# Cross-attention with image prompts: where the context is transposed, and how the last heads' prompts reach the output

## The chip, the core and the metric

The kernel runs on one core of a Trainium2 chip. The metric is device time of one execution, in microseconds (us); lower is better. The engines are named as the profile names them: PE is TensorE (PEld its weight loads), DVE is VectorE, ACT is ScalarE, POOL is GpSimd, and SP is SyncE, which here only issues DMAs.

## The reference

Everything is fp32. There are B = 8 batches, S = 112 queries of C = 320 channels, H = 20 heads of 16 channels, and a context of 375 tokens of E = 512 features. The first 371 tokens are text, the last 4 are image prompts.

```
text_ehs, ip_ehs = ehs[:, :-4], ehs[:, -4:]
q = heads(x @ W_q); k_t = heads(text_ehs @ W_k); v_t = heads(text_ehs @ W_v)
probs_t  = softmax(q @ k_t^T * 16**-0.5)
text_out = probs_t @ v_t
k_ip = heads(ip_ehs @ W_k_ip); v_ip = heads(ip_ehs @ W_v_ip)
qsem = l2norm(probs_t @ text_ehs)              # one 512-vector per query and head
sem  = qsem @ l2norm(ip_ehs)^T
probs_ip = softmax(q @ k_ip^T * 16**-0.5 + 0.5 * sem) * spatial_mask
out = (text_out + probs_ip @ v_ip) @ W_out + b_out + x
```

The context holds one batch in (8, 375, 512); the mask has one number per query.

## The kernel before

**What is computed per step.** A step is one pair (batch b, group g); a batch has five groups of four heads. The kernel never forms qsem. It keeps, per batch, the matrix of inner products of all context tokens with each other (the gram matrix G, text and normalised prompts) in a buffer `u`, with a column of ones and the values v of each head beside it. For each head, `multiplied` (L641) computes p^T times [G | prompts | 1 | v] on PE, where p are the unnormalised probabilities: 12 blocks of 32 tokens for four heads, so 48 matmuls a step, in four PSUM banks `ps_qd`. `reduced` (L687, DVE) multiplies the first 371 columns with p and sums them, which is the squared length of qsem; `value_sums` (L654, ACT) copies the last 21 columns (four prompt products, the sum of p, 16 channels of p times v).

**What makes p.** `scores` (L592, PE) computes one head's scores two steps ahead (LEAD = 2): heads 2 and 3 behind product block 0 of a step, heads 0 and 1 behind block 6. `probabilities` takes the maximum on DVE (nmx, L605), the exponential on ACT (p, L609), and sends p by a DMA on SP's queue into `xg`, with 28-row pieces; `transposed` (L622) then turns `xg` into `xgT` by one DVE transpose of 128x1536, which works in squares of 32x32, and PE loads `xgT` as weights in the next step's products. The order of DVE in a step is: nmx of heads 2 and 3, xgT, nmx of heads 0 and 1, four reductions.

**What stands between two steps.** Behind each step's products, `between(b, g)` issues PE work for the next batch nb = b + 1 and closes batch b - 1. Generators are advanced by pieces with `run`. Before the change the PE order behind the products of batch b is:

| g | PE work behind the products |
|---|---|
| 0 | three gram blocks of nb (L415) |
| 1 | values of nb, token blocks 0 and 1 (L486) |
| 2 | values of nb, token block 2; key block 0 (L453) |
| 3 | key block 1; in odd b transposes of x for a pair of batches; key block 2 (three PE transposes of `k3`, L444); transposes of attn (`ps_a`, L845); in even b queries (L305) |
| 4 | context transposes of nb + 1, first token block (`ps_c`, L357); output projection of b - 1 (`ps_o`, L858); context transposes, blocks 1 and 2; queries |

**The context.** `load_ctx(b)` reads a batch's 375x512 floats into `ct` with token rows on partitions, in four DMAs of up to 128 rows. It is called by `load_next(b + 2)` behind the step (b, 0). `transposed_context` turns `ct` into `ctxT` (features on partitions) by four PE transposes per token block through a PSUM bank, copied out by ACT. The gram, the keys and the values all read `ctxT`. `load_embed` loads the weights W_k, W_v and the prompt weights so that feature e * 128 + p lies in row p of block e. POOL fills the last columns of `ctxT` (memset in `begin`) and copies the normalised prompts into its columns 371 to 374 (in `gram`).

**Closing a batch.** `finish(b)` runs in ten pieces while the next batch is computed: the root of the squared lengths (ACT), the fused prompt scores and their softmax (DVE and ACT), w (L771, DVE), then on POOL the product of w with the prompt values `vip` (wv, L827), two sums (L838, L839) and the last sum into `attn` (L840). Then come PE transposes of attn (`ps_a`), an ACT copy (aT), the output projection (`ps_o`), DVE's sum with x and bias (`ob`), and the store.

**What sets the order.** PE, SP, DVE and, behind the prologue, ACT run in the order in which the program issues the work. POOL's order is made by a scheduler up to the last batch, and by hand in it. PSUM has eight banks: four `ps_qd`, two `ps_sc` (the scores; `bank(..., spare=True)` borrows from them), two `ps_mm` (the rest). A tile of a ring must wait until the tile that held the place before has been read.

**The last batch and the end.** The last batch, b = 7, has no next batch, so its work is shared between ACT, POOL and DVE (`shared`), and its heads close in two parts: `finish(b, (0, 16), bd=...)` for the first 16 heads, and `finish(b, (16, 20), nc.vector, late=True)` for the last group. The first part does not multiply w with prompt values. It transposes w (`ps_wT`) and multiplies it on PE with `bd`, a matrix with the prompt values of each head in that head's channels, into the same bank as the transposes of attn. The second part multiplies w with `vip` on DVE, adds the sum to attn and then transposes. `awake(3, end=True)` issues three idle matmuls before the last reductions.

Of the kernel before, what the change touches and what calls it, by code (L numbers as in the profile page):

```python
# [14 lines left out]
NIP = 4  # L15
# [5 lines left out]
def kernel(  # L21
# [36 lines left out]

    GROUP = 4
# [54 lines left out]
    def load_embed(eng, t, w):  # L114
        eng.dma_start(t[:, :, :C], w.rearrange("(e p) f -> p e f", p=P))
# [7 lines left out]

    def load_ctx(b):
        ct = io.tile([P, NT, E], F32, tag="ct", name=f"ct_{b}")
        for c in range(NT):
            rows = min(P, T - c * P)
            some = rows - rows % 16
            nc.sync.dma_start(ct[:some, c, :], ehs[b, c * P : c * P + some, :])
            if some < rows:  # L130
                nc.sync.dma_start(ct[some:rows, c, :], ehs[b, c * P + some : c * P + rows, :])
        return ct
# [82 lines left out]
    def normalised_prompts():  # L215
# [16 lines left out]
        for src, dst, n in ((ipn, ipnT, "n"), (ip_sb, ipT, "r")):  # L232
            ps = bank(f"ps_ipT{n}")
            for e in range(NE):
                nc.tensor.transpose(
                    ps[:, e * N : (e + 1) * N], src[:, e * P : (e + 1) * P], ident[:N, :N]
                )
            nc.vector.tensor_copy(
                dst, ps[:, : NE * N].rearrange("p (e n) -> p e n", n=N)
            )  # L240
# [87 lines left out]
    def begin(b):  # L328
        s = st[b] = dict(ct=loaded.pop(b))
        s["ctxT"] = work.tile([P, NE, TP], F32, tag="ctxT", name=f"ctxT_{b}")  # L330
        nc.gpsimd.memset(s["ctxT"][:, :, T:], 0.0)

        s["kT"] = work.tile([P, NC, T], F32, tag="kT", name=f"kT_{b}")
        s["vext"] = work.tile([P, NT, C + REST], F32, tag="vext", name=f"vext_{b}", bufs=1)
# [14 lines left out]
    def transposed_context(b):  # L349
        begin(b)  # L350
        s = st[b]
        ct, ctxT = s["ct"], s["ctxT"]
        for c in range(NT):
            rows = min(P, TT - c * P)
            ps = bank(f"ps_c_{b}_{c}", spare=b > 1 and c > 0)
            for e in range(NE):
                nc.tensor.transpose(  # L357
                    ps[:, e * P : e * P + rows],
                    ct[:rows, c, e * P : (e + 1) * P],
                    ident[:rows, :rows],  # L360
                )
# [72 lines left out]
    def keys(b):  # L434
# [3 lines left out]
        for i in range(NC):  # L438
            ps = bank(f"ps_k_{b}_{i}")
# [39 lines left out]
    def values(b):  # L479
        s = st[b]  # L480
        ctxT, vext = s["ctxT"], s["vext"]
# [201 lines left out]
    def reduced(b, g, a0=0):  # L683
        s = st[b]
        for a, (h, ps) in list(enumerate(zip(groups[g], s["qd", g])))[a0:]:
# [11 lines left out]
        del s["p", g]  # L697
# [5 lines left out]
    def finish(b, heads=(0, H), eng=None, late=False, bd=None):  # L703


        s = st[b]
        eng = eng or nc.gpsimd
# [14 lines left out]
        if not late:  # L722
            if "xb" not in s:
                s["xb"] = work.tile([S, C], F32, tag="xb", name=f"xb_{b}", bufs=1)
                with_bias(b)
# [86 lines left out]
        else:  # L812
            yield from prompt_sums_and_projection(
                b, s, eng, part, n, h0, h1, i0, i1, w, attn, ah, late
            )
# [9 lines left out]
    def prompt_sums_and_projection(b, s, eng, part, n, h0, h1, i0, i1, w, attn, ah, late):  # L825
# [7 lines left out]
        if late:  # L833
            ips = small.tile([S, GROUP, D], F32, tag="ips", name=f"ips_{b}", bufs=1)
            nc.vector.tensor_reduce(ips, wv.rearrange("p n h d -> p h d n"), AX.X, ALU.add)
            nc.vector.tensor_tensor(ah, ah, ips, ALU.add)
        else:
            eng.tensor_tensor(wv[:, :2], wv[:, :2], wv[:, 2:], ALU.add)  # L838
            eng.tensor_tensor(ah, ah, wv[:, 0], ALU.add)  # L839
            eng.tensor_tensor(ah, ah, wv[:, 1], ALU.add)  # L840
        yield

        ps = bank(f"ps_a_{b}_{h0}", spare=not late)
# [10 lines left out]
        if not late:  # L854
            s["o"] = bank(f"ps_o_{b}")
        ps = s["o"]
        for i in range(i0, i1):
            nc.tensor.matmul(  # L858
                ps[:S, :C], aT[:, i, :], wo_sb[:, i, :], start=(i == 0), stop=(i == NC - 1)
            )  # L860
        yield
# [7 lines left out]
    LEAD = 2  # L869
# [11 lines left out]
    def between(b, g):  # L881
# [26 lines left out]
        if g == 3:  # L908
            if new:
                run(("k", nb), None, 1)  # L910
            for bs in first if b > 0 else ():
                run(("q", bs[0]), lambda: project_queries(bs), 3)
            if b == 0:
                run(("t", b), lambda: prompt_logits(b))
            if nb < B - 1:
                run(("k", nb), None, 1)
            if b > 0 and new:
                run(("f", b - 1), None)
            for bs in rest:
                run(("q", bs[0]), None)  # L920
        if g == 4:
            if nb + 1 < B:
                run(("c", nb + 1), lambda: transposed_context(nb + 1))
            if b > 0 and new:
                run(("f", b - 1), None, 2)
            if nb + 1 < B:
                run(("c", nb + 1), None, 2)
# [51 lines left out]
    for n, (b, g) in enumerate(steps[:-NG]):  # L979
# [27 lines left out]
        if g == 0:  # L1007
            load_next(b + 2)
        elif g == 1:
# [39 lines left out]
    for g in range(NG):  # L1049
# [34 lines left out]
        if g == 1:  # L1084
            prompt_values(b)
# [4 lines left out]
        if g == 3:  # L1090
# [5 lines left out]
            for _ in range(3):  # L1096
                next(first)
    next(first)
    run(before, None)
    nc.scalar.preload_act_table(AF.Sqrt)  # L1100
    run(before, None)
    awake(3, end=True)
    run(before, None)
    reduced(b, g)
    value_sums(b, g)
    last = finish(b, (FULL * HC, H), nc.vector, late=True)
# [3 lines left out]
    next(first)  # L1110
    for _ in range(2):
        next(last)
    for _ in range(2):
        next(first)
    for _ in range(4):
        next(last)
    drain(gens[before])
    drain(first)
# [44 lines left out]
```

## Time and profile before

| what | value |
|---|---|
| median of 3 runs | 448.66 us (448.07 to 451.15) |
| the profiled execution | 449.23 us |
| its span from the first to the last record | 447.5 us |
| group products, PE L641 | 3840 matmuls, 217.9 us busy |
| all matmuls of PE | 5095 |
| nmx, DVE L605 | 160 of 529 ns |
| reductions, DVE L687 | 148 of 542 ns |
| exponentials, ACT L609 | 160 of 582 ns |
| wv, POOL L827 | 6 of 2461 ns |

The steps of a middle batch take PE 10.64, 10.72, 10.64, about 9.8 and 9.55 us for g = 0 to 4, some 51.3 us a batch. Of each step the 48 products with the four scores inside them take 5.37 us. The end, behind the last product at 432.9 us, runs through DVE's last reductions (to 435.97), the root on ACT with a table load (to 438.12), two rounds of transposes and projection on PE (to 444.13), the sum (444.65) and the store (447.5).

In the page, part 1 gives each engine's busy time, part 4 the shares of the chain that ended last, and part 5 the costliest groups: line, engine, operation, output<-input, count, then busy time and mean of one, then the idle time before them and what ended it. In the chain in order of time, a line gives the start, the length, the engine, the work and its line; in an engine's timeline, a line gives start, length, the instruction, and in brackets the idle time before it with what ended it.

### The profile page before, as it was taken

What the parts mean: (1) busy time and instruction counts of PE and PEld (TensorE: products, weight loads), DVE (VectorE), ACT (ScalarE), POOL (GpSimd) and SP (SyncE); (2) the same over time, 40 slices, a digit from 0 to 9 for tenths busy, and PEclk for the clock granted to TensorE, in tenths of its full rate; (3) what the DMA queues carried; (4) which work ended last, traced back from release to release, by engine and by line L of the source; (5) the groups of instructions that cost most, each with busy time, mean ns of one, the idle gap of its engine ahead of it and who ended that gap; (6) DMA issues with size and microseconds to landing.
All of it is one profiled execution on the core that took longest, in us unless ns stands there. A gap on an engine that the chain in (4) does not pass through costs nothing.

```text
span 447.5 us, 13078 instructions
## 1 busy us (share of the span) xinstructions
PE 435.1 (97%) x5095; PEld 336.3 (75%) x5095; DVE 308.9 (69%) x649; ACT 196.5 (44%) x664; POOL 111.1 (25%) x270
## 2 busy tenths in 40 slices
PE   8998999999999999999999999999999999999885
PEld 8756767888778876788777777778777887787782
DVE  4047356787687767786687866776677867878784
ACT  2254232435345353343535463333534454446782
POOL 4302201011150111511142121511133120527420
PEclk9999999999999999999999999999999999999998
DMA  7669955544645566544646466464556437454400
GB/s 237 174 170 259 212 138 141 141 136 139 171 123 135 145 171 167 128 130 142 167 123 158 117 174 163 129 158 149 141 159 147 137 87 196 123 134 112 136 2 26
DMA packets 52159, 64.84 MB, mean 145 GB/s; under 512 B 18370, under 2 KB 44146, under 8 KB 52098
## 3 DMA queue, kind: packets, MB, share of 16 engines
q1 hardware_dynamic: 51658, 63.45, 53.1%
q8 instruction: 40, 0.66, 0.7%
q10 hardware_dynamic: 440, 0.56, 0.4%
q14 instruction: 21, 0.17, 0.1%
HBM read 19.30 MB, written 5.32 MB: 55 GB/s over the span
## 4 chain that ended last, share of the span: by engine, by line
PE 86%; DVE 4%; ACT 4%; DMA 3%; issue 1%; POOL 1%; SPq 1%; DVEq 0%; POOLq 0%; ACTq 0%
PE ps_qd L641 39%; PE ps_v L486 13%; PE ps_g L415 8%; PE ps_k L453 8%; PE ps_s L592 4%; PE ps_q L305 3%; PE ps_o L858 3%; DMA xg<-p 3%; PE ps_c L357 2%; DVE xgT L622 2%; ACT p L609 2%; PE ps_g L387 1%; DVE junk L687 1%; PE ps_w L374 1%; PE ps_k L469 1%
## 5 line engine op out<-in xcount | busy, mean ns | idle before, releaser
L641 PE MATMUL ps_qd<-u,xgT 32*112 32x104 f32 (+11 forms) x3840 | 217.9, 352 | 3.4 <-DVE xgT L622 1.2
L641 PEld LDWEIGHTS ps_qd<-u,xgT 32*112 32x112 f32 x3840 | 185.8, 172 | 36.7 <-issue 10.3
L605 DVE TENSOR_REDUCE nmx<-ps_s 112x1 f32<-112x371 f32 x160 | 77.6, 529 | 72.4 <-PE ps_s L592 72.3
L622 DVE STREAM_TRANSPOSE xgT<-xg 128x1536 f32<-128x1536 f32 x40 | 119.0, 2976 | 8.0 <-DMA xg<-p 7.4
L609 ACT ACTIVATE p<-ps_s,nmx 112x371 f32<-112x371 f32 x160 | 86.9, 582 | 80.7 <-DVE nmx L605 58.0
L687 DVE CUSTOM_DVE_ANT_0 junk<-ps_qd,p 112x371 f32<-112x371 f32 x148 | 80.2, 542 | 15.8
L559 POOL COPY u<-vr 128x64 f32<-128x64 f32 x120 | 25.8, 236 | 163.9 <-PE ps_qd L641 106.5
L592 PE MATMUL ps_s<-kT,qm 32*112 32x375 f32 (+1 forms) x320 | 64.8, 481 | 0.4 <-ACT p L609 0.4
L486 PE MATMUL ps_v<-wv_sb,ctxT 128*128 128x384 f32 (+1 forms) x192 | 63.5, 480 | 0.0
L486 PEld LDWEIGHTS ps_v<-wv_sb,ctxT 128*128 128x128 f32 x192 | 35.2, 190 | 19.7
L453 PE MATMUL ps_k<-ctxT,wk_sb 128*128 128x371 f32 x136 | 45.9, 482 | 0.0
L654 ACT COPY pvs<-ps_qd 112x21 f32<-112x21 f32 x150 | 16.0, 188 | 64.3 <-PE ps_qd L641 63.4
L415 PE MATMUL ps_g<-ctxT 128*128 128x375 f32 (+2 forms) x168 | 37.4, 379 | 0.0
L453 PEld LDWEIGHTS ps_k<-ctxT,wk_sb 128*128 128x128 f32 x136 | 25.1, 190 | 15.3 <-issue 0.5
L415 PEld LDWEIGHTS ps_g<-ctxT 128*128 128x128 f32 x168 | 28.1, 190 | 8.4
L592 PEld LDWEIGHTS ps_s<-kT,qm 32*112 32x112 f32 x320 | 25.9, 170 | 5.7 <-ACT kT L460 2.1
L314 DVE TENSOR_SCALAR qm<-ps_q,emask 128x224 f32<-128x224 f32 (+1 forms) x25 | 9.2, 400 | 23.6 <-PE ps_q L305 23.6
L611 ACT COPY ipl<-ps_s 112x4 f32<-112x4 f32 x140 | 23.5, 168 | 0.0
L493 ACT COPY vext<-ps_v 128x384 f32<-128x384 f32 (+1 forms) x24 | 11.2, 466 | 25.4 <-PE ps_v L486 25.4
L460 ACT COPY kT<-ps_k 128x371 f32<-128x371 f32 x17 | 8.0, 470 | 25.3 <-PE ps_k L453 25.3
L403 ACT ACTIVATE ug<-ps_g 128x375 f32<-128x375 f32 (+2 forms) x24 | 9.0, 376 | 22.4 <-PE ps_g L415 17.9
L827 POOL TENSOR_TENSOR wv<-vip,w 112x1280 f32<-112x1280 f32 x6 | 14.8, 2461 | 14.6 <-DVE w L771 14.6
(131 smaller groups left out, 336.4 us busy)
## 6 DMA issues: line engine op xcount, KB each, us to landing
xg<-p SPq DMA_DIRECT2D x160, 162.3 KB
u<-ug SPq DMA_DIRECT2D x128, 99.0 KB
ct<-in_ctx_dram SPq DMA_DIRECT2D x16, 256.0 KB
vip<-vipd SPq DMA_DIRECT2D x7, 560.0 KB
vr<-vd SPq DMA_DIRECT2D x32, 120.0 KB
vd<-vext SPq DMA_DIRECT2D x7, 320.0 KB
ct<-in_ctx_dram SPq DMA_DIRECT2D x8, 224.0 KB
vd<-vext SPq DMA_DIRECT2D x7, 160.0 KB
```

The lines of the kernel that those rows point to most:

```text
L415: nc.tensor.matmul(ps[:, : T - t0], ctxT[:, e, t0 : t0 + P], ctxT[:, e, t0:T], start=(e == 0), stop=(e == NE - 1),)
L453: nc.tensor.matmul(ps[:, :TT], wk_sb[:, e, i * P : (i + 1) * P], s["ctxT"][:, e, :TT], start=(e == 0), stop=(e == NE - 1),)
L486: nc.tensor.matmul(ps[:, :w], ctxT[:, e, c * P : (c + 1) * P], wv_sb[:, e, :w], start=(e == 0), stop=(e == NE - 1),)
L559: nc.gpsimd.tensor_copy(region(b, c)[:, :, UV - c * P :], s["vr"][:, c * QN : (c + 1) * QN, g, :])
L592: nc.tensor.matmul(ps[:S, :w], qm[a * RG : (a + 1) * RG, i, r, j * S : (j + 1) * S], s["kT"][a * RG : (a + 1) * RG, i, :w], start=True, st ...
L605: nc.vector.tensor_reduce(nmx, ps[:S, :TT], AX.X, ALU.max, negate=True)
L609: nc.scalar.activation(p, ps[:S, :TT], AF.Exp, bias=nmx)
L611: nc.scalar.copy(s["ipl"][:, groups[g][a], :], ps[:S, TT:T])
L622: nc.vector.transpose(xT.rearrange("p j (k q) -> p q j k", q=QN), xg.rearrange("p q (j k) -> p q j k", k=RG),)
L641: nc.tensor.matmul(banks[a][:S, j * RG : UW], xT[a * RG : (a + 1) * RG, j, :S], region(b, c)[a * RG : (a + 1) * RG, q, q * RG :], start=(j ...
L654: nc.scalar.copy(s["pvs"][:, h, :], ps[:S, TT:UW])
L687: nc.vector.tensor_tensor_reduce(out=junk, in0=ps[:S, :TT], in1=s["p", g][:, a, :], scale=1.0, scalar=0.0, op0=ALU.mult, op1=ALU.add, accu ...
```

## The change

**The context of batches 2 to 7 is turned by DVE.** `load_ctx(b)` for b >= 2 lays the context out in squares: row i of a quarter a holds, for each of 12 blocks j of 32 tokens, token 32 j + i's features 128 a to 128 a + 127. That takes four DMAs of 32 x 11 x 128 floats and four of 19 x 128 for the last tokens, in pieces of 512 bytes, and a POOL memset of the last block. `transposed_context` for b >= 2 then issues three DVE transposes of 128x512, one per 128 tokens, that read every fourth element of a row; no PE transposes and no ACT copies are left there. Feature e + 4 p now lies in row p of block e, so `load_embed` loads the weights in that order, and the PE transposes that remain (contexts 0 and 1, and the prompts) read their input with a step of four elements (`chunk`).

**The places in `between` move.** The DVE transposes stand behind g = 0, 1 and 2 (g = 1, 2 and 3 in b = 0) instead of PE's in g = 4. In g = 3 the piece of `finish(b - 1)` that issues `ps_a` goes ahead of key block 1. Key block 2 moves from g = 3 to g = 4, behind `ps_o`, and takes a spare bank. The load of a context is issued behind (b, 4) for batch b + 3, with one first call behind (0, 0) for batch 2, instead of behind (b, 0) for batch b + 2. The memset of the padding in `ctxT` is left out for b >= 2, since the transposes write those columns.

**The last heads' prompts go through the projection on their own.** `projected_prompts` multiplies the last four heads' block of `bd` with W_out's last rows ahead of time (`bw`, 16 x 320). `last_heads` then adds to the output bank two matmuls: attn of the last heads (without prompts) times W_out, and w transposed times `bw`. The three idle matmuls at the end, the load of `vip` for the last batch and the `late` branch of `finish` go. The last reductions are issued in two parts, one before and three behind other work, and the ACT copies of the last products stand ahead of them.

```diff
 def load_embed(eng, t, w):
-    eng.dma_start(t[:, :, :C], w.rearrange("(e p) f -> p e f", p=P))
+    eng.dma_start(t[:, :, :C], w.rearrange("(p e) f -> p e f", e=NE))
...
+def chunk(t, e):
+    return t.rearrange("t (p e) -> t e p", e=NE)[:, e, :]
 def load_ctx(b):
     ct = io.tile([P, NT, E], F32, tag="ct", name=f"ct_{b}")
+    if b >= LEAD:
+        v = ct.rearrange("p c e -> p (c e)").rearrange("p (j f) -> p j f", f=P)
+        full = TT // RG
+        nc.gpsimd.memset(v[:, full, :], 0.0)
+        for a in range(QN):
+            nc.sync.dma_start(
+                v[a * RG : (a + 1) * RG, :full, :],
+                ehs[b, : full * RG, a * P : (a + 1) * P].rearrange("(j i) f -> i j f", i=RG),
+            )
+        for a in range(QN):
+            nc.sync.dma_start(
+                v[a * RG : a * RG + TT - full * RG, full, :],
+                ehs[b, full * RG : TT, a * P : (a + 1) * P],
+            )
+        return v
...
 def begin(b):
-    nc.gpsimd.memset(s["ctxT"][:, :, T:], 0.0)
+    if b < LEAD:
+        nc.gpsimd.memset(s["ctxT"][:, :, T:], 0.0)
...
 def transposed_context(b):
+    if b >= LEAD:
+        for c in range(NT):
+            some = slice(c * QN, (c + 1) * QN)
+            nc.vector.transpose(
+                ctxT[:, :, c * P : (c + 1) * P].rearrange("p e (j i) -> p j e i", i=RG),
+                ct[:, some, :].rearrange("p j (k e) -> p j e k", e=NE),
+            )
+            yield
+        return
     for c in range(NT):
-        ps = bank(f"ps_c_{b}_{c}", spare=b > 1 and c > 0)
+        ps = bank(f"ps_c_{b}_{c}")
...
 def keys(b):
-        ps = bank(f"ps_k_{b}_{i}")
+        ps = bank(f"ps_k_{b}_{i}", spare=0 < b < B - 1 and i == FULL)
...
+def projected_prompts(bd):
+    k0 = FULL * HC * NIP
+    k = HN - k0
+    ps = bank("ps_bT", spare=True)
+    nc.tensor.matmul(ps[:REST, :k], bd[k0:HN, FULL * P : C], ident[k0:HN, k0:HN], start=True, stop=True)
+    bT = work.tile([P, NC, S], F32, tag="aT", name="bT")
+    nc.scalar.copy(bT[:REST, 0, :k], ps[:REST, :k])
+    yield
+    ps = bank("ps_bw", spare=True)
+    nc.tensor.matmul(ps[:k, :C], bT[:REST, 0, :k], wo_sb[:REST, FULL, :], start=True, stop=True)
...
+    nc.scalar.copy(bw, ps[:k, :C])
+    yield
+def last_heads(b):
...
+    nc.scalar.activation(rn, rn, AF.Sqrt)
+    nc.scalar.preload_act_table(AF.Exp)
+    yield
...
+    nc.vector.scalar_tensor_tensor(w, ex, sm_sb, over_ip(rx), ALU.mult, ALU.mult)
+    yield
+    ps = bank(f"ps_a_{b}_{h0}")
+    nc.tensor.transpose(ps[:, :S], attn[:, FULL * P :], ident[:S, :S])
+    aT = work.tile([P, NC, S], F32, tag="aT", name=f"aT_{b}_{h0}")
+    nc.scalar.copy(aT[:, FULL, :], ps[:, :S])
+    nc.tensor.matmul(s["o"][:S, :C], aT[:, FULL, :], wo_sb[:, FULL, :], start=False, stop=False)
+    yield
+    k = n * NIP
+    ps = bank(f"ps_wT_{b}_{h0}")
+    nc.tensor.transpose(ps[:k, :S], w.rearrange("s h n -> s (h n)"), ident[:S, :S])
+    wT = small.tile([S, S], F32, tag="wTl", name="wT_last", bufs=1)
+    nc.scalar.copy(wT[:k], ps[:k, :S])
+    nc.tensor.matmul(s["o"][:S, :C], wT[:k], s["bw"], start=False, stop=True)
...
 def between(b, g):
     if g == 3:
+        if b > 0 and new:
+            run(("f", b - 1), None)
         if new:
             run(("k", nb), None, 1)
         for bs in first if b > 0 else ():
             run(("q", bs[0]), lambda: project_queries(bs), 3)
         if b == 0:
             run(("t", b), lambda: prompt_logits(b))
-        if nb < B - 1:
-            run(("k", nb), None, 1)
-        if b > 0 and new:
-            run(("f", b - 1), None)
         for bs in rest:
             run(("q", bs[0]), None)
+    if 0 <= g - (b == 0) < NT and nb + 1 < B:
+        run(("c", nb + 1), lambda: transposed_context(nb + 1))
     if g == 4:
-        if nb + 1 < B:
-            run(("c", nb + 1), lambda: transposed_context(nb + 1))
         if b > 0 and new:
             run(("f", b - 1), None, 2)
-        if nb + 1 < B:
-            run(("c", nb + 1), None, 2)
+        if nb < B - 1:
+            run(("k", nb), None, 1)
...
-    if g == 0:
+    if n == 0:
         load_next(b + 2)
-    elif g == 1:
+    if g == NG - 1:
+        load_next(b + 3)
+    if g == 1:
         gram_to_groups(b + 1, (1,))
...
+value_sums(b, g)
 next(first)
+late = projected_prompts(bd[:, 1])
 run(before, None)
+next(late)
+run(before, None)
+next(late)
+reduced(b, g, 0, 1)
+next(first)
+next(first)
 nc.scalar.preload_act_table(AF.Sqrt)
 run(before, None)
-awake(3, end=True)
-run(before, None)
-reduced(b, g)
-value_sums(b, g)
-last = finish(b, (FULL * HC, H), nc.vector, late=True)
+reduced(b, g, 1)
+next(first)
+last = last_heads(b)
```

## The prediction

> **What bounds the kernel now.** I read the page's busy times first, then the chain that ended last in order of time, then the timelines of POOL and DVE around one batch's end. One step is one pair (batch b, group g); steps of a batch differ only in what PE does behind its 48 group products.
>
> ```profile
> PE 435.1 (97%) x5095; PEld 336.3 (75%) x5095; DVE 308.9 (69%) x649; ACT 196.5 (44%) x664; POOL 111.1 (25%) x270
> ...
> PE 86%; DVE 4%; ACT 4%; DMA 3%; issue 1%; POOL 1%; SPq 1%; DVEq 0%; POOLq 0%; ACTq 0%
> ```
>
> PE is never idle for long between 37 and 405 us, so PE time removed there is worth its full length, unless a wait takes its place. The chain through g = 3 and g = 4 of batch 4:
>
> ```profile
> 286.55 2.69 PE ps_k L453 x8
> 289.24 0.32 PE ps_k L444 x3
> 289.56 0.29 PE ps_a L845 x3
> 289.85 1.35 PE ps_q L305 x6
> ...
> 296.56 0.59 PE ps_c L357 x4
> 297.15 1.61 PE ps_o L858 x6
> 298.77 0.83 PE ps_c L357 x8
> 299.60 1.15 PE ps_q L305 x6
> ```
>
> Columns are start, length, work. The reader is to see the order: in g = 3 (PE from 281.18; products end at 286.55) the second key block comes first and the transposes of attn (ps_a) come 3.0 us later, at 289.56; in g = 4 the context transposes cost 0.59 + 0.83 = 1.42 us. What ps_a reads is made by POOL:
>
> ```profile
> 281.56 2.46 POOL L827 TENSOR_TENSOR wv<-vip,w 112x1280 f32<-112x1280 f32 x1 [1.95 <-DVE w L771]
> 284.10 1.55 POOL L838 TENSOR_TENSOR wv<-wv 112x640 f32<-112x640 f32 x1
> 285.73 0.87 POOL L839 TENSOR_TENSOR attn<-attn,wv 112x320 f32<-112x320 f32 x1
> 286.68 0.86 POOL L840 TENSOR_TENSOR attn<-attn,wv 112x320 f32<-112x320 f32 x1
> ```
>
> attn is whole at 287.54: 0.99 us after the products, 2.0 us before PE now asks for it. And DVE at the end of g = 2, with the row of its nearest relative:
>
> ```profile
> 281.18 0.30 DVE L771 SCALAR_TENSOR_TENSOR w<-ex,sm_sb,rx 112x80 f32<-112x80 f32 x1
> 282.70 1.00 DVE L605 TENSOR_REDUCE nmx<-ps_s 112x1 f32<-112x371 f32 x2 [1.22 <-PE ps_s L592]
> ...
> L622 DVE STREAM_TRANSPOSE xgT<-xg 128x1536 f32<-128x1536 f32 x40 | 119.0, 2976 | 8.0 <-DMA xg<-p 7.4 <-issue 0.6
> ```
>
> DVE idles 1.22 us there, waiting for the next step's scores. The same gaps before nmx are 2.95 us behind g = 0 (261.34) and 3.26 us behind g = 1 (272.07).
>
> **Part 1: PE loses the context transposes of batches 2 to 7.** They stand in g = 4 of b = 0 to 5. For b = 1 to 5: 5 x 1.42 = 7.1 us off PE. In b = 0 the chain shows 2.18 us (91.73 to 93.91, a bank wait of 0.50 in it), but there g = 4 would shrink below what DVE allows: its fourth reduction, which frees the bank that PE's fourth product of the next step writes, ends 8.65 us after the step's start (299.85 against 291.20 in b = 4), and PE issues that product 0.35 us into its step, so a step is at least 8.3 us. Step (0, 4) takes 8.74 now: 0.4 gained, and 0.35 in (0, 3), from where the last key block (0.32) moves to (0, 4). Together 0.75. For b >= 1, g = 4 becomes 5.36 products + 1.61 ps_o + 0.32 key transposes + 1.15 queries = 8.44 us, just above 8.3: no stall, with 0.1 us to spare. ACT loses three copies of 0.6 us a batch, hidden anyway (44% busy). **-7.85 us.**
>
> **Part 2: DVE takes three transposes of 128x512 a batch.** The row is xgT: 2976 ns for 1536 elements, so 992 ns each. Behind g = 0 and g = 1 they fit the gaps of 2.95 and 3.26. Behind g = 2 the piece runs from about 281.5 to 282.5, and the maxima come at 282.7: hidden, with 0.2 us left. Cost 0 so long as one takes under 1.2 us. Bounds: 0.68 us (the other 371-element DVE rows, nmx at 529 ns, scaled by 512/371 to 0.73, with little fixed cost) and 3 us. [...] I take the row, since xgT has the same step on its other side, and keep +3 for the range. The same step now stands in the PE weight loads of contexts 0 and 1 and of the prompts (32 loads; 140 ns each now). No row has such a load; between 0 and one more load each, mostly beside matmuls: 0 taken, +2 kept.
>
> **Part 3: g = 3 asks for attn first.** In `between`, finish(b-1) now precedes the keys, so ps_a stands directly behind the products. PE is in order: keys and queries queue behind it. attn is not earlier: DVE's w and POOL's chain start where they did. L840 ends behind the products by 0.88, 0.95, 0.95, 0.99, 0.93 us in b = 1 to 5 and 1.38 in b = 6 (POOL timelines against the chain's 132.54, 183.76, 235.32, 286.55, 338.11, 388.07): 6.1 us. Into that POOL chain, behind the first product, the new order puts the copy of the normalised prompts into ctxT (0.20; its DVE piece ends at 282.5, before L827 does, so it does not wait) in b = 1 to 5 and the memset of the next context's last block (0.20) in b = 1 to 3; with 0.05 between, 3 x 0.5 + 2 x 0.25 = 2.0 us. ps_a also takes a scores bank, free when ACT has read head 0, 6.4 us into the step: about when attn comes, so no more. **+8.1 us.** The bank wait stays as a floor of 1.05 us a batch should POOL be faster. While PE waits nothing else of PE's can run; what follows slips with it. What was given in g = 4 is taken in g = 3, and b = 6 pays without having gained.
>
> **Part 4: transfers.** A context now comes in 8 transfers, of 512-byte pieces, issued behind (b, 4) for b+3 rather than behind (b, 0). SP: 8 x 0.47 (the median of vr's issues, of the same shape) = 3.8 us where 4 took 1.7. They and the prompts' load (0.53) start some 8.1 us into g = 4 (144.93 in b = 1) and end 12.5 us in, when the next heads' p has been ready for about 1.3 us; those are heads 2 and 3, whose xg is followed by heads 0 and 1, 4 us later, and xgT waits for the last. POOL's memset runs a step earlier, so SP does not wait for it. Data: vr moves 1536 pieces of 320 bytes in about 3 us with the queues 87% busy (137.0 to 139.3), so 1484 pieces of 512 bytes take 3 to 5 us; they are needed 9 us into the next step, 5 us after they land. Cost 0; uncovered, up to 1 us a batch at xgT. The prompts' load dropped from the last batch (413.73, no one waited) is worth 0. The weights' layout changes which rows a partition holds; in the prologue PE runs through from 1.4 to 27 us, so 0.
>
> **Part 5: the end.** Now, behind the last product (432.9): four reductions to 435.97, then ACT's root, a table load of 1.28 to 438.12, wT, ps_a, aT, two ps_o groups and DVE's sum to 444.65. After: ACT reads pvs before the reductions, the first 16 heads' weights are done about 2.3 us earlier (434.8 against 437.4), and the last heads skip 1.3 us of DVE (L827, L835, L836). Against this, PE gets bT, bw (about 0.6) and one more ps_o (0.6), and ACT's root for the last heads stands behind aT of the first 16, at about 439.2, with a load of 1.28 behind it. Adding up by rows: last ps_o ends between 443.0 and 444.0, where it ends at 444.13 now. -0.6, between -1.1 and +0.5; the three idle matmuls that go (L374) may let the clock, 0.66 from 440 and 0.50 from 442, fall sooner.
>
> **Sum.** -7.85 + 8.1 - 0.6 = -0.35. The profiled execution took 449.23 (span 447.5 and 1.7 around it); it would take 448.9. It lies 0.57 above the median of the runs, so I say **448.4 us**.
>
> **Rivals.**
> 1. ps_a does not wait: POOL's chain is found earlier, or PE later. For it: nothing but that the margin is small, 1 us. Against: the order is fixed and both ends are in the trace. The time would be 448.66 - 7.85 - 0.6 = 440.2. Chance 0.11.
> 2. Slower: the transpose behind g = 2. It delays maxima, p and scores from 1.2 us of length on. At a whole xgT (2.98) it is 1.75 us late; PE stalls 1.1 us in the products, head 0's p and with it the bank for ps_a come at 8.2 instead of 6.75 us: 1.45 x 5 + 1.1, 8.3 us, 456.7. From about 2.3 us of length it costs 1%. [...] Chance 0.13 of something between 451.5 and 457.
> 3. The transfers come late at (b, 0): 1 us x 6, 454. For it: double the SP time in a step 1.1 us shorter. Against: 5 us of cover. Chance 0.05.
> 4. The forecast: 0.71, between 446 and 450.5.
>
> **How the numbers follow.** About 1% is what a measurement of this kernel can tell from no change: below 444.2 and above 453.1. Rival 1 gives faster, with little more from a better end: 0.13. Slower takes two thirds of rivals 2 and 3 and something unseen: 0.17. Same 0.70. The range 444.0 to 453.0 holds the forecast with the +3 and +2 kept above, and leaves out rival 1 and half of rival 2.
>
> **What would show it.** PE: idle of 1.2 to 1.5 us before ps_a in g = 3 of b = 1 to 6, released by POOL's last sum; no ps_c behind (0, 4). DVE: 18 transposes of about 1.0 us, the gap before nmx behind g = 2 down to about 0.2. The step g = 4 at 8.4 us and g = 3 at 10.6 to 10.9. I am wrong if ps_a finds attn ready, if the new transposes exceed 1.3 us, or if xgT waits for xg in g = 0 or 1.

## The result: 1% slower, and the profile after

| | before | after |
|---|---|---|
| median of 9 runs each | 448.56 us (447.54 to 451.15) | 452.64 us (451.61 to 453.30) |
| ratio, 95% interval | | 1.0096 (1.0082 to 1.0110) |
| span of the profiled execution | 447.5 us | 451.4 us |

The forecast was 448.4 us, a hair faster. The time lies inside the range (444 to 453), but the change made the kernel slower, clear of noise: with nine runs of each, the 1% that the forecast called the least that can be told apart is known to 0.14%. From the page of the changed kernel, first the busy times and then the shares of the chain that ended last:

```profile
PE 430.0 (95%) x5024; PEld 332.4 (74%) x5024; DVE 325.2 (72%) x664; ACT 189.1 (42%) x649; POOL 111.4 (25%) x270
...
PE 63%; DVE 13%; POOL 8%; DMA 5%; ACT 4%; issue 4%; SPq 3%; DVEq 0%; POOLq 0%; ACTq 0%
```

PE is busy 5.1 us less and the kernel takes 3.9 us longer, so PE waits about 9 us more. PE's share of the chain fell from 86% to 63%. DVE and POOL are on it now, and the chain of b = 4 says where. Columns are start, length, work:

```profile
281.70 0.31 DVE w L802
282.02 0.07 issue
282.09 2.46 POOL wv L856
284.55 0.14 POOL ctxT L441
284.70 1.52 POOL wv L862
286.21 0.07 issue
286.28 0.88 POOL attn L863
287.17 0.07 issue
287.23 0.07 POOL attn L864
287.30 0.73 issue
288.03 0.25 POOL u L591
288.28 0.47 PE ps_a L869 x3
288.75 2.51 PE ps_k L484 x8
291.26 1.14 PE ps_q L326 x6
292.40 1.15 PE ps_qd L673 x10
```

The path runs through DVE's w and POOL's five instructions into ps_a, and key block 1 and the queries stand behind it. The chain names what came last by the profile. A second thing comes at nearly the same time: ps_a takes a bank of the scores, which is free when ACT has read head 0. Here attn is whole at 288.09 and ACT's last read of that bank ends at 288.17:

```profile
288.02 0.15 ACT L643 COPY ipl<-ps_s 112x4 f32<-112x4 f32 x1
```

In PE's timeline each ps_a has idle time before it (in brackets, with what ended it), one line for each of b = 1 to 6:

```profile
134.43 0.48 PE L869 MATMUL ps_a<-ident,attn 112*128 112x112 f32 x3 [1.18 <-POOL attn L864]
...
185.80 0.51 PE L869 MATMUL ps_a<-ident,attn 112*128 112x112 f32 x3 [1.58 <-POOL attn L864]
...
237.33 0.51 PE L869 MATMUL ps_a<-ident,attn 112*128 112x112 f32 x3 [1.19 <-POOL attn L864]
...
288.28 0.48 PE L869 MATMUL ps_a<-ident,attn 112*128 112x112 f32 x3 [1.16 <-POOL u L591]
...
341.16 0.48 PE L869 MATMUL ps_a<-ident,attn 112*128 112x112 f32 x3 [2.56 <-issue]
...
392.46 0.51 PE L869 MATMUL ps_a<-ident,attn 112*128 112x112 f32 x3 [1.42 <-POOL attn L864]
```

The sum is 9.09 us. In b = 2, 3 and 6 attn comes last (1.53, 1.14 and 1.36 us behind the products), in b = 1 and 4 ACT's read (1.07 and 1.06, where attn has 1.04 and 0.97). The fifth is of another kind, and it is looked at below.

The whole difference of the two profiled executions, by steps. A step's length is the distance from its first group product to that of the next step, read from PE's timeline of each kernel:

| steps | before | after | difference |
|---|---|---|---|
| start to the first step | 36.67 | 37.52 | +0.85 |
| (0, 3) and (0, 4) | 19.15 | 18.42 | -0.73 |
| g = 4 of b = 1 to 6 | 55.69 | 50.73 | -4.96 |
| g = 0 of b = 1 to 6 | 63.93 | 65.80 | +1.87 |
| g = 3 of b = 1 to 6 | 57.98 | 65.34 | +7.36 |
| g = 1 and 2 of b = 1 to 6, and (0, 0) to (0, 2) | | | 0.0 |
| the last batch up to its last step | 28.39 | 28.59 | +0.20 |
| from the last step's first product to the end | 19.64 | 18.93 | -0.71 |
| sum | | | +3.88 |

So g = 4 gave 5 us, g = 3 took 7.4, and g = 0, for which the forecast put nothing, took 1.9.

### The profile page after: what moved, and what is told of

It is laid out like the page before. It is cut to its first block, busy times and chain, and to the rows that moved or that the text cites. A ratio compares the mean times of both kernels' runs of the same rounds, so it can differ in the third digit from the quotient of the medians.

```text
span 451.4 us, 12959 instructions
## 1 busy us (share of the span) xinstructions
PE 430.0 (95%) x5024; PEld 332.4 (74%) x5024; DVE 325.2 (72%) x664; ACT 189.1 (42%) x649; POOL 111.4 (25%) x270
## 4 chain that ended last, share of the span: by engine, by line
PE 63%; DVE 13%; POOL 8%; DMA 5%; ACT 4%; issue 4%; SPq 3%; DVEq 0%; POOLq 0%; ACTq 0%
PE ps_qd L673 26%; PE ps_g L446 8%; PE ps_v L518 7%; PE ps_k L484 5%; DVE xgT L654 5%; DVE junk L719 3%; PE ps_s L624 3%; PE ps_q L326 3%; PE ps_o L881 2%; DMA u<-ug 2%; POOL wv L856 2%; DVE nmx L637 2%; POOL wv L862 2%; ACT p L641 2%; DMA xg<-p 1%
## 5 line engine op out<-in xcount | busy, mean ns | idle before, releaser
L673 PE MATMUL ps_qd<-u,xgT 32*112 32x328 f32 (+11 forms) x3840 | 219.5, 352 | 3.4 <-DVE xgT L654 1.3
L673 PEld LDWEIGHTS ps_qd<-u,xgT 32*112 32x112 f32 x3840 | 187.4, 172 | 35.8 <-issue 10.3
L624 PE MATMUL ps_s<-kT,qm 32*112 32x375 f32 (+1 forms) x320 | 66.7, 484 | 0.4 <-ACT p L641 0.4
L484 PE MATMUL ps_k<-ctxT,wk_sb 128*128 128x371 f32 x136 | 47.0, 491 | 0.0
L378 DVE STREAM_TRANSPOSE ctxT<-ct 128x512 f32<-128x512 f32 x18 | 19.9, 1104 | 0.0
```

Of the source, the lines that this page charges most:

```text
L378: nc.vector.transpose(ctxT[:, :, c * P : (c + 1) * P].rearrange("p e (j i) -> p j e i", i=RG), ct[:, some, :].rearrange("p j (k e) -> p j ...
L484: nc.tensor.matmul(ps[:, :TT], wk_sb[:, e, i * P : (i + 1) * P], s["ctxT"][:, e, :TT], start=(e == 0), stop=(e == NE - 1),)
L624: nc.tensor.matmul(ps[:S, :w], qm[a * RG : (a + 1) * RG, i, r, j * S : (j + 1) * S], s["kT"][a * RG : (a + 1) * RG, i, :w], start=True, st ...
L673: nc.tensor.matmul(banks[a][:S, j * RG : UW], xT[a * RG : (a + 1) * RG, j, :S], region(b, c)[a * RG : (a + 1) * RG, q, q * RG :], start=(j ...
```

## The experiments

Ten kernels were run. Each time stands beside runs of the kernel before on the same chip, 447.94 us in the first four, 448.16 in the next four, 448.68 in the last two (448.56 beside the changed kernel). Where two changed kernels of different series are compared, some tenths of a microsecond lie in that.

**1. The order of g = 3 taken back (e1).**

```diff
 if g == 3:
-    if b > 0 and new:
-        run(("f", b - 1), None)
     if new:
         run(("k", nb), None, 1)
     ...
+    if b > 0 and new:
+        run(("f", b - 1), None)
     for bs in rest:
```

> The changed kernel with the transposes of attn (ps_a) behind key block 1 and the transposes of x again, in g = 3; everything else stays. Theory A (the waits for attn are the loss): the six idle times before ps_a (1.18, 1.58, 1.19, 1.16, 2.56, 1.42 us, 9.1 in all) go, and the half clock after the longest one with them (about 1.6); 452.6 - 10.7 = 442, faster than both kernels; steps g = 3 at 9.2 (odd b) and 9.7 (even b). Rival B (the loop DVE to POOL to PE bounds the kernel now: its chain has 13% DVE and 8% POOL): the time given back in g = 3 comes up as waits in g = 4 and g = 0, and the result stays above 447.

446.18 us, ratio 0.9955 (0.9940 to 0.9971). Faster than both kernels, by 6.5 us than the changed one, but 4 us short of theory A. Its chain is PE's again:

```profile
PE 86%; DMA 4%; ACT 4%; DVE 4%; issue 1%; POOL 1%; SPq 0%; DVEq 0%; ACTq 0%
```

No ps_a waits for attn or for a bank of the scores. What stayed away lies in three places. In odd b, ps_a stands 0.57 us waiting for ACT's copy of xT, whose bank it takes. The steps g = 0 keep their 0.2 us and more over the 10.64 of the kernel before. And (4, 4), (5, 0), (5, 3), (5, 4) and (6, 0) are 2.6 us longer in sum than their like, behind an xgT that starts late (it waits 0.68 us for xg in (4, 4), 1.71 in (5, 3), 1.27 in (5, 4)). Theory A holds for the waits. Rival B's figure was not reached either, but some of the time did come up in g = 4 and g = 0, though without POOL.

**2. The order of g = 3 alone, in the kernel before (e2).**

```diff
 if g == 3:
+    if b > 0 and new:
+        run(("f", b - 1), None)
     if new:
         run(("k", nb), None, 1)
     ...
-    if b > 0 and new:
-        run(("f", b - 1), None)
```

> The kernel before with one move alone: in g = 3 the piece that issues ps_a goes ahead of key block 1 (PE still turns the context). Theory A: PE idles 1.1 to 1.5 us before ps_a in b = 1 to 4 and 6, and 2.5 to 3 in b = 5, where the bank comes late, with a half clock behind it: +5 to +6 and +4.5, so about 458 to 459. Rival B (the waits come from POOL's inserted copies, the transfers or DVE's transposes of the change): below 452.

456.23 us, ratio 1.0182 (1.0164 to 1.0200), 8.3 us more. One move of a few lines costs all that. The idle times before ps_a are 1.16, 1.16, 1.15, 1.16, 2.51 and 1.45 us, nearly those of the changed kernel, though attn is whole 0.88 to 0.99 us behind the products in b = 1 to 5: in b = 1 to 4 it is the bank that sets them (ACT's read ends 1.05 to 1.07 behind). All this comes without POOL's inserted copies, without DVE's transposes and with the old transfers. Two of them from PE's timeline of this kernel, for b = 1 and b = 5:

```profile
133.90 0.48 PE L845 MATMUL ps_a<-ident,attn 112*128 112x112 f32 x3 [1.16 <-POOL u L559]
...
345.58 0.79 PE L845 MATMUL ps_a<-ident,attn 112*128 112x112 f32 x3 [2.51 <-issue]
```

Rival B is out. In the profile the steps g = 3 cost 10.3 us more and (5, 4) gives 0.6 of it back; the profiled execution was the longest of the six, 458.54 us.

**3. The step of 16 bytes alone, in the kernel before (e3).**

```diff
-    eng.dma_start(t[:, :, :C], w.rearrange("(e p) f -> p e f", p=P))
+    eng.dma_start(t[:, :, :C], w.rearrange("(p e) f -> p e f", e=NE))
...
-    ct[:rows, c, e * P : (e + 1) * P],
+    chunk(ct[:, c, :], e)[:rows],
```

> The kernel before with one part alone: features in the order e + 4p, so that all PE transposes of contexts and prompts load their weights with a step of 16 bytes; no DVE transposes. In the changed kernel such a load takes 214 ns where it took 140, and the first step began 0.85 us later. Theory A (the start is late for these loads): the first step begins 0.85 us late here too, and the 72 loads of the loop show some 0.02 to 0.07 us each, so 1.4 to 5 more: 451 to 454. Rival B (the start is late for the weights' own transfers or the second load of the first call): the start is not later, and each loop load still costs, or everything is hidden: 448.6.

449.88 us, ratio 1.0046 (1.0030 to 1.0063). The loads are longer. Rows by form of PE's weight loads, with busy time and mean ns behind the first bar, in the kernel before:

```profile
L357 PEld LDWEIGHTS ps_c<-ident,ct 115*128 115x128 f32 x32 | 3.4, 140 | 0.5 <-DVE ipnT L238 0.2
```

and in e3:

```profile
L360 PEld LDWEIGHTS ps_c<-ident,ct 115*128 115x128 f32 x32 | 4.5, 214 | 0.1
```

The 64 loads of 128 rows go from 150 to 208 ns. Most of this lies beside matmuls: the steps (1, 4) to (4, 4) take 9.75 us instead of 9.55, 17 ns a load, and the steps from the first to the last are 0.63 us longer in sum. The start is no later: the first step begins at 36.43 us. Theory A's reason for the late start falls, and B's too. Over all twelve profiles the first step begins between 36.19 and 37.53 us: the nine with strided loads at 36.95 in the mean, the three without at 36.93. So the 0.85 in the table above lies within the scatter from one execution to the next. Of the 2 us that the medians show, more than half is thus not found in the trace of this run.

**4. One transfer moved (e4).** vipx is a DRAM to DRAM transfer of 205 KB that lays out the prompt values for the last two batches; both kernels issue it behind (5, 1).

```diff
-    if (b, g) == (B - 3, 1):
+    if (b, g) == (B - 3, 3):
         prompt_values_by_head()
```

> The changed kernel with the transfer that spreads the last prompts' values (vipx) issued behind (5, 3) and not (5, 1). Theory A: this transfer makes xg of (5, 3) late (SP waits 0.8 us for it, and xgT starts 1.4 us late, in the kernel before as well), so head 0's probabilities and with them the bank of ps_a; with it moved, the idle time before ps_a in b = 5 falls from 2.56 to 1.2 us, PE's clock stays whole there, and the time falls by 3 us to 449.6; the lateness moves to (6, 0), where there is slack. Rival B (the lateness comes from other transfers of b = 5): nothing changes, 452.6.

449.90 us, 2.7 less than the changed kernel, with ratio 1.0043 (1.0027 to 1.0060) to the kernel before. The step (5, 3) falls from 12.89 to 9.80 us, and the idle time before ps_a from 2.56 to 1.16. What had happened there, from the timeline of the changed kernel:

```profile
337.10 2.98 DVE L654 STREAM_TRANSPOSE xgT<-xg 128x1536 f32<-128x1536 f32 x1 [1.35 <-DMA xg<-p]
339.92 0.93 DVE L637 TENSOR_REDUCE nmx<-ps_s 112x1 f32<-112x371 f32 x2
340.44 0.57 ACT L641 ACTIVATE p<-ps_s,nmx 112x371 f32<-112x371 f32 x1 [1.40 <-DVE nmx L637]
340.91 0.16 ACT L643 COPY ipl<-ps_s 112x4 f32<-112x4 f32 x1
...
341.16 0.48 PE L869 MATMUL ps_a<-ident,attn 112*128 112x112 f32 x3 [2.56 <-issue]
```

attn was whole at 339.59. ps_a went at 341.16, just behind ACT's last read of head 0's scores, whose bank it takes. ACT was late because the maxima were, behind an xgT that started 3.93 us into the step where 2.50 is the rule, for lack of xg. In the kernel before, xgT of (5, 3) was just as late (3.83 us in), from DVE's timeline of that kernel:

```profile
336.50 3.00 DVE L622 STREAM_TRANSPOSE xgT<-xg 128x1536 f32<-128x1536 f32 x1 [1.24 <-DMA xg<-p]
```

ps_a did not wait for it there, since it came 3.9 us behind the products. It was not free either: the products of (5, 4) took 6.04 us instead of 5.44. Nor does the place of vipx make xgT late each time: in the profile of the run of the end alone (8), with vipx at its old place, xgT of (5, 3) waited 0.01 us, and (5, 4) took 9.08 us instead of 9.68. In the changed kernel the wait had a second price. Its windows (stretch, its length, busy time of PE, PEld, DVE, ACT, POOL with counts, then granted clock, DMA share and GB/s):

```profile
338.60:341.10 2.50, 0.00 (x0) 0.00 (x0) 2.50 (x4) 1.07 (x7) 1.44 (x5) 1.00 0.78 192
341.10:343.00 1.90, 1.84 (x7) 1.27 (x8) 1.47 (x7) 0.93 (x3) 0.00 (x0) 0.84 0.29 64
343.00:345.00 2.00, 2.00 (x5) 1.07 (x4) 0.41 (x2) 0.00 (x0) 0.00 (x0) 0.50 0.71 191
345.00:347.00 2.00, 2.00 (x17) 1.16 (x19) 0.00 (x0) 0.91 (x4) 0.00 (x0) 0.80 0.85 186
```

PE stood still for 2.5 us, and its granted clock then went to 0.50, from 342.4 to 345.8 us: the eight matmuls of key block 1 took 4.28 us, where in e4, with the clock at 1.00, they took 2.67. So (5, 3) lost 1.4 us by the longer wait and 1.6 by the clock.

**5. DVE's context transposes twice (e5).**

```diff
+    for _ in range(2):
         nc.vector.transpose(
             ctxT[:, :, c * P : (c + 1) * P].rearrange("p e (j i) -> p j e i", i=RG),
             ct[:, some, :].rearrange("p j (k e) -> p j e k", e=NE),
         )
```

> The changed kernel with each of DVE's context transposes issued twice (1.10 us more behind g = 0, 1 and 2 of each batch). Theory A (Part 2: hidden by DVE's gaps, which are 1.8 and 2.2 us wide behind g = 0 and 1 with one transpose in them, and 0.22 behind g = 2): nothing is lost behind g = 0 and 1; behind g = 2 the maxima come 0.9 us late, and with them head 0's probabilities and the bank for ps_a, so PE idles some 0.6 us more there: +3, about 455.5. Rival B (DVE's load as such is the loss of the change): 3.3 us of DVE a batch show in full, +15 to +20. Rival C (nothing of DVE is on the path in g = 3, attn alone is): 452.6.

456.85 us, ratio 1.0188 (1.0166 to 1.0209), 4.2 more than the changed kernel: near A's 3, far from B's 15 to 20. The steps g = 0 and 1 of b = 1 to 6 stay within 0.1 us of what they were. The loss is 1.1 us each in (0, 3) and (0, 4), of which A said nothing, and 0.2 to 0.8 in each g = 3 of b = 1 to 5, 2.7 us in sum. So rival C is out too. The place within g = 3 is another than A said: the wait before ps_a grows only from 1.2 to 1.3 us, and it is the stretch of the products, with the scores inside it, that grows (in b = 1 from 5.4 to 6.0 us). The run shows one thing more. With products so long, attn is whole well before ps_a is issued, and ps_a waits all the same. From the timelines of POOL, ACT and PE of this kernel in b = 3, where the products end at 238.84:

```profile
238.33 0.86 POOL L865 TENSOR_TENSOR attn<-attn,wv 112x320 f32<-112x320 f32 x1
...
239.86 0.15 ACT L644 COPY ipl<-ps_s 112x4 f32<-112x4 f32 x1
...
240.11 0.48 PE L870 MATMUL ps_a<-ident,attn 112*128 112x112 f32 x3 [1.27 <-POOL u L592]
```

attn has been there for 0.9 us, and ps_a follows ACT's read by 0.1. An earlier attn alone would not take the waits away.

**6. ps_a directly behind key block 1, and vipx later (best1).**

```diff
+if new:
+    run(("k", nb), None, 1)
 if b > 0 and new:
     run(("f", b - 1), None)
-if new:
-    run(("k", nb), None, 1)
 for bs in first if b > 0 else ():
...
-    if (b, g) == (B - 3, 1):
+    if (b, g) == (B - 3, 3):
```

> The changed kernel with ps_a directly behind key block 1 in every batch (in e1 it stood behind the transposes of x in odd b and waited 0.57 us for ACT's copy of them), and with vipx issued behind (5, 3). Theory A: odd steps g = 3 lose the 0.57 (three of them), and (5, 3), (5, 4) and (6, 0), which are 0.5, 0.5 and 1.0 us longer than their like in e1, become as the others: 446.2 - 1.7 - 2.0 = 442.5. Rival B (with steps g = 3 this short, xg of the next step comes late, as xgT's 0.68 us of idle in (4, 4) of e1 hints): the gain of g = 3 comes back in g = 4 and g = 0, 444 to 446.

445.91 us, ratio 0.9956 (0.9939 to 0.9972): no better than e1. The odd steps gave 0.34 each, but vipx now met the load of vip behind (5, 4), and xgT of (6, 0) waited as no other, from DVE's timeline of this kernel:

```profile
353.09 2.97 DVE L654 STREAM_TRANSPOSE xgT<-xg 128x1536 f32<-128x1536 f32 x1 [3.30 <-DMA xg<-p]
```

(6, 0) took 12.11 us, (6, 1) 10.21. Rival B's figure is right. Its reason holds for (4, 4), where xgT idled 1.00 us; (6, 0) is another matter.

**7. The fourth reduction of g = 4 shortened, in best1 (floor).**

```diff
+            w = 16 if g == NG - 1 and a == GROUP - 1 and b < B - 2 else TT
             nc.vector.tensor_tensor_reduce(
-                out=junk, in0=ps[:S, :TT], in1=s["p", g][:, a, :],
+                out=junk[:, :w], in0=ps[:S, :w], in1=s["p", g][:, a, :w],
```

> best1 with the fourth reduction of g = 4 (b = 0 to 5) over 16 columns and not 371: it leaves out most of one head's squared length. Theory A (the steps g = 4 and g = 0 are held by DVE: its fourth reduction ends 8.8 us after the step's start, and PE's fourth product of the next step waits for its bank): the reduction is about 0.35 us shorter, so (b, 4) and (b + 1, 0) together fall from 19.47 to about 19.1 us, and the time by 5 x 0.35 = 1.8 us against best1. Rival B (PE's own work or the transfer of xg holds these steps): the same time as best1.

This kernel leaves out most of one head's squared length. 445.07 us, ratio 0.9923 (0.9897 to 0.9948). The totals can't tell it from best1, whose interval touches. In the profile, the longest of the six executions, (6, 0) and (6, 1) came 2.4 us longer: xgT of (6, 0) waited 4.40 us for xg, and PE's clock fell after an idle time, from PE's timeline and from windows with the columns as above:

```profile
357.48 1.15 PE L446 MATMUL ps_g<-ctxT 128*128 128x119 f32 x8 [1.75 <-ACT ug L434]
...
358.60:361.90 3.30, 3.30 (x24) 3.16 (x27) 0.94 (x5) 0.27 (x1) 0.46 (x1) 0.50 0.36 106
```

The steps can: (1, 4) with (2, 0) and (2, 4) with (3, 0) fall from some 19.45 to 19.26 us, and g = 0 is back at 10.64; (1, 0) falls from 11.35 to 10.98. (3, 4) with (4, 0) came 0.24 longer, since xgT of (3, 4) waited 0.53 us for xg there and the reductions with it; again (4, 0) lost what the fourth reduction entered it by (0.32 for 0.28). So DVE held g = 0, by 0.2 us in most batches of best1. The other 0.2 that g = 4 lacks is PE's own, since (1, 4) and (2, 4) stay at 8.63.

**8. The end alone, in the kernel before (tail_alone).** Its diff is the last part of the change's diff, with the two new functions; all edits to contexts, to the weights' order and to `between` are left out.

> The kernel before with the end of the changed kernel alone (the last heads' prompts through the projection on their own, the reductions in two parts, no idle matmuls, no load of vip for the last batch); contexts and the order of g = 3 as before. Theory A (Part 5): -0.6 us, 447.4 against 448.0. Rival B: the second table load and the two small extra matmul groups eat it: no difference or +0.5. From the profiles so far the stretch from the last step's first product to the end was 19.64, 19.15 and 19.05 us with the old end, 18.93, 19.27 and 18.69 with the new one, which can't tell.

447.83 us against 448.16, ratio 0.9992 (0.9984 to 1.0000): between 0.7 us gained and nothing. Its profile shows 19.27 us from the last step's first product to the end, within the scatter of both kinds.

**9. vipx in the first batch (best2), or on ACT's queue (best3).** Both have ps_a directly behind key block 1. The first piece is best2's, the second best3's.

```diff
-    if (b, g) == (B - 3, 1):
+    if (b, g) == (0, 1):
...
-        nc.sync.dma_start(vipx, ...
+        nc.scalar.dma_start(vipx, ...
```

> The changed kernel with ps_a directly behind key block 1 in every batch, and vipx issued behind (0, 1), where the steps are 11.8 us long and DVE needs 8.8 to 9. Theory A: its place sets its cost; in best1 it met the load of vip behind (5, 4), and xgT of (6, 0) waited 3.3 us for xg, so that (6, 0) and (6, 1) took 1.28 and 0.34 us more than their like. Here nothing of PE's waits: (5, 3) at 9.3, (6, 0) at 10.8, (6, 1) at 9.87, the time 445.9 - 1.6 = 444.3. Rival B (xg of (6, 0) is late for other transfers, vipx only coincides): (6, 0) stays at 11.8 or more, 445.5 to 446.

> The same kernel as best2, but with vipx at its old place behind (5, 1) and issued on ACT's queue instead of SP's. Theory A (what makes xg late in (5, 3) is SP's own queue, which stood 0.8 us for vipx's place in it): xgT of (5, 3) starts 2.5 us into the step again, 444.3. Rival B (it is the data of vipx among the 16 engines that holds xg's data up): xgT of (5, 3) starts at 3.3 or later, and (5, 3), (5, 4) and (6, 0) stay long as in e1, 446.

best2 took 445.54 us, ratio 0.9925 (0.9905 to 0.9945), the lowest of the kernels that leave nothing out, though its interval touches those of e1, best1 and best3. (5, 3) is 9.24 and (6, 1) 9.87 as expected, but (0, 3) pays 1.4 us: its xgT waits 2.42 us for xg, which it does in no other kernel, and PE then stands 1.43 us for ACT's copy of keys. And (6, 0) stays at 11.66, where xg was not late: (5, 4) is only 8.15 long there, and DVE's fourth reduction ends 0.98 us into (6, 0). So the 1.6 us were not to be had, and for (6, 0) neither theory was right. best3 took 446.53 us, ratio 0.9956 (0.9942 to 0.9970). xgT of the step before, (5, 2), waited 2.70 us, so that (5, 3) took 11.23. In this profile, keeping vipx out of SP's queue does not take the lateness away; it comes a step sooner, as ACT issues the transfer in (5, 1), at 315.2 us, where SP issues it in (5, 2). That it is the data of vipx which holds xg up was not looked at by itself.

## Why the prediction was wrong

The forecast said -7.85 for Part 1, +8.1 for Part 3, -0.6 for Part 5 and 0 for the rest, -0.35 in all (which makes 448.3 and not 448.4 us). The profiles have +3.9. The main mechanism was the right one: a wait before ps_a in g = 3 eats what g = 4 gives. The sum failed by two terms. The larger error in it comes from one step of the reasoning that was wrong and not only mis-sized: that g = 4 can shrink to 8.44 us without a stall in g = 0.

**Part 1 was too large by 2.4 us,** 1.9 of it in g = 0 and 0.5 in g = 4. It failed at "just above 8.3: no stall, with 0.1 us to spare", and at 8.44 for PE's own work.

The g = 4 steps of b = 1 to 4 are 8.63 or 8.73 us, because what now stands first behind the products, ps_o, takes 1.80 us instead of 1.61. The chain shows the same elsewhere: before, the first context piece took 0.59 for four transposes and the other two 0.83 for eight; key block 1 took 2.69 directly behind the products and takes 2.51 behind ps_a. In these cases the first work behind the 32-row products pays about 0.18 us, whichever it is, so that removing it saves 0.18 less than its row says.

And the next step, g = 0, stalls. The forecast let the fourth reduction end 0.35 us into the next step for free. It also read that end as 8.65 us after the step's start; with start and end taken as in the table below it is 8.79 in (4, 4) of the kernel before. Measured, from the timelines of DVE and PE (before had 10.64 for these steps where no stall is):

| step | its length | end of its fourth reduction | into the next step by | next step over 10.64 |
|---|---|---|---|---|
| (0, 4) | 8.33 | 9.00 | 0.67 | 0.71 |
| (1, 4) | 8.73 | 8.81 | 0.08 | 0.12 |
| (2, 4) | 8.63 | 8.79 | 0.16 | 0.20 |
| (3, 4) | 8.73 | 8.80 | 0.06 | 0.10 |
| (4, 4) | 8.63 | 8.80 | 0.17 | 0.20 |
| (5, 4) | 8.18 | 8.78 | 0.60 | 0.64 |

All of the time by which the reduction enters the next step is lost, and 0.03 to 0.05 us more; there is no free third of a microsecond. The length from which g = 4 costs the next step nothing is 8.8 us and not 8.3. In (1, 0) the timeline of the changed kernel shows the wait itself:

```profile
95.24 0.55 DVE L719 CUSTOM_DVE_ANT_0 junk<-ps_qd,p 112x371 f32<-112x371 f32 x1
...
95.84 0.17 PEld L673 LDWEIGHTS ps_qd<-u,xgT 32*112 32x112 f32 x1 [0.43 <-DVE ss L719]
```

PE's weight load stands 0.43 us for the reduction that ended at 95.79. In the batches with 0.1 or 0.2 us no idle time is recorded, only a score product that takes longer. The run floor shows that the reduction is the cause there too; by which path it holds the scores up stays open.

**Part 3 was about right in sum, by two errors of opposite sign.** It had +8.1. With the 0.32 us a batch for key block 2, which Part 1 counts, the runs have 7.36 + 1.6 = 9.0. Five batches took 5.3 where the forecast's working gives them 6.9. POOL's inserted copies were put at 2.0 in all. They delay attn by 0.15 us in b = 1 and 0.19 in b = 3, most of it within the wait for the bank; the 0.58 us more in b = 2 come mostly from DVE's w, which is 0.4 late there, behind a reduction of (2, 2) that stood 0.52 us (why is open). The rest is small: in odd b, key block 2 took 0.58 us in g = 3 with a short wait for ACT's copy of xT, where 0.32 was counted, and key block 1 takes 0.18 less; in even b the queries take 1.14 us instead of 1.35.

The sixth batch, b = 5, took 3.6 where 1.2 was in the sum. The step that failed is "ps_a also takes a scores bank, free when ACT has read head 0, 6.4 us into the step: about when attn comes, so no more". That time holds in b = 1 to 4 and 6; in b = 5 it was 7.7 us in the kernel before already. The trace of before had xgT of (5, 3) 1.3 us late, in plain sight of DVE's timeline, but mostly hidden by the order that the change gives up. That PE's granted clock would be at 0.50 behind the wait of 2.56 us (1.6 us lost) was not in the sum at all.

**Part 2 was right.** 18 transposes of 1104 ns each (992 taken, 1200 allowed), and the gap before the maxima behind g = 2 is 0.30 us in b = 1 and 0.22 to 0.24 in b = 3 to 5; in b = 2 there is none, and the maxima start 0.07 us later:

```profile
281.92 1.11 DVE L378 STREAM_TRANSPOSE ctxT<-ct 128x512 f32<-128x512 f32 x1
283.27 1.00 DVE L637 TENSOR_REDUCE nmx<-ps_s 112x1 f32<-112x371 f32 x2 [0.24 <-PE ps_s L624]
```

An element that was read with a step of 16 bytes took 2.16 ns (1104 ns for the 512 of a row), one that was written so 1.94 (xgT, 2976 for 1536). No run shows the +3 us that the forecast kept in its range for the transposes: at 1104 ns they stayed under the 1.2 us that it allowed, and of the maxima behind them in b = 1 to 5 only those of b = 2 came later, by 0.07 us. No run transposes without that step on either side, so what the step costs on DVE stays open; on PE it shows, where the load of weights of 115 rows goes from 140 ns (kernel before) to 214 (e3). Rival 2's price, 1% lost from about 2.3 us of length, is met by e5 only in total: 2.2 us at all three places lost 0.9%, but 2.3 of the 5.1 us that its steps lost lie in b = 0, of which rival 2 said nothing.

**Part 4** was right in that no step g = 0 of b = 1 to 5 waits for xg; SP did wait 4.8 us in all, at the issues of xg, until transfers of contexts had landed, under cover. **Part 5** is -0.7 in the two profiles and -0.36 (-0.7 to 0) by the run of the end alone: of the right sign if it is anything.

What remains is the start, 0.85, which is within the scatter of single executions, and 0.2 in the last batch. The terms that were missed, 2.4 + 0.9 + 0.85 + 0.2 - 0.1, are the 4.25 us between -0.35 and +3.9. So the forecast came as near as it did partly by luck: within Part 3 a shortfall of 1.6 stands against an excess of 2.4.

Rival 1 named the right cure: without the wait the kernel is faster (e1). Its 440.2 was too low mainly by Part 1's error, by what (4, 4) to (6, 0) lose, and by the 0.57 us that odd b wait for xT.

## What to carry to other kernels

Where work is taken off the bounding engine in a step, ask first how much shorter the step can become before another engine holds it, and measure that limit from several steps, start to start. A wait must be read at its worst step, not at a typical one: what is late but covered in one place before (here xg of one step) becomes the bound as soon as the order gives up its cover. And an in-order engine should ask last for what a slow chain delivers: the same three transposes wait for no attn behind key block 1, and standing in front of it they cost 6.5 us in the changed kernel and 8.3 in the one before.

## What the runs showed of the hardware

- PE's granted clock went to 0.50 for 3.4 us after PE had stood idle for 2.56, 2.51, 2.14 and 1.75 us (changed kernel, e2, e5, floor), and stayed at 1.00 after 1.58 (changed kernel, b = 2). Where the limit lies, and whether it is the length of one stop alone, no run shows.
- The first full-height matmuls behind the 32-row products took about 0.18 us longer than the same matmuls in another place (ps_o 1.80 us in the changed kernel against 1.61 in the one before, key block 1 2.69 in the one before against 2.51 in the changed). What the 0.18 us are, no run shows: none changed the height of the matmuls alone.
- Where one transfer of 205 KB within DRAM was issued, xgT of the next step waited for xg: 1.35 us (changed kernel, on SP's queue in (5, 2)), 2.70 (best3, on ACT's in (5, 1)), 2.42 (best2, in (0, 2)), 2.03 and 3.30 (e4 and best1, in (5, 4), beside the load of vip). The wait moved with the transfer, but its size did not hold: in the run of the end alone it was 0.01, with the transfer in the same place as in the changed kernel.
